# Half of the products of the squares of 16 on GpSimd, one of its folds a step earlier, and the gate's remainders by TensorE and ScalarE

## The chip, the cores and the metric

One core of a Trainium2 chip runs the whole program. The metric is the device time of one execution in microseconds; lower is better. The engines are TensorE (PE in the profile, with its weight loads as PEld), VectorE (DVE), ScalarE (ACT), GpSimd (POOL) and SyncE (SP), whose queue only issues transfers. [...]

## The reference

A block of four layers over x of shape (8, 512, 256) in fp32, each behind a layer norm and added to x:

```
x = x + attn_a(layernorm(x))     # 16 heads of 64; attention inside one token
x = x + ffn(layernorm(x))        # 256 -> 1024 -> 1024 -> 1024 -> 256
x = x + attn_b(layernorm(x))     # 16 heads of 16, causal over the 512 tokens
x = x + ffn(layernorm(x))        # the same weights again
```

Attention A is the unusual part. For every token and head, q, k and v are vectors of 64 numbers, the scores are their outer product, masked causally, and the softmax goes over the 64 channels:

```
scores[q, k] = Q[q] * K[k] / 8,  k <= q        # 64 x 64 for each token and head
attn[q] = sum_k softmax(scores)[q, k] * V[k]
```

No matrix product computes these scores; they are elementwise work. The feed-forward net is `h = silu(x W1) * (x W2)`, two layers with GELU, and W3.

## The kernel before, in words

**Squares.** Tokens lie in the partitions, 128 at a time. The causal triangle of 64 x 64 is cut into squares below the diagonal: one of 32, two of 16, four of 8 and so on, and the diagonal. A *group* is 128 tokens and 4 heads; there are 8 batches x 4 groups of heads x 4 tiles of tokens = 128 groups. A group has four *units*, `u`:

- u=0: the squares of 32 of heads 0 and 1 (tile `w`, three buffers)
- u=1: the squares of 16 of all four heads (tile `w16`, one buffer; the trace names it `w` too)
- u=2: the squares of 32 of heads 2 and 3 (`w`)
- u=3: the squares of 8, 4, 2 and 1 (`ws`, one buffer)

One unit goes through these stages:

- `scores` (L784): the products q*k, 2 x 1024 elements in each partition for u=0, 1, 2. GpSimd makes them for u=0 and 2, VectorE for u=1 and 3.
- `exps` (L798): ScalarE's exponential, one instruction for a unit.
- `weigh` (L808): VectorE multiplies by v into the second half of each part of the tile.
- `halve` (L814): a transfer, issued by GpSimd, adds the second 2048 columns of a tile onto the first 2048 (1024 KB). Not for u=3.
- `fold` (L819): GpSimd adds 1024 columns onto 1024, for u=0 and 2 only.
- `gather` (L845): VectorE's sum over the columns left, into a small tile `red`; for u=1 it reads the 2048 columns themselves.
- `add_rows` (L852): GpSimd adds `red` to the group's accumulator `acc`.

At the end of a group VectorE takes the reciprocal of the denominators (`invert`, L856), GpSimd multiplies (`divide`, L860), and TensorE turns and projects the result.

**Order.** The order on TensorE, VectorE, ScalarE and GpSimd is written out by hand: `AttentionA.step(n)` issues, for step n, the stages of the units n, n-1, n-2 and so on, in three parts with a `yield` after each. So four steps make a group. Counting steps by the unit that begins in them (s0 to s3), `gather` of u=1 stands at the end of part 1 of s1, the `add_rows` for it, `small_squares` and the fold of u=2 follow on GpSimd in part 2 of s1, and `gather` of u=2 stands in part 3 of s2. The fold of u=0 stands in part 2 of the next group's s0, its `gather` in part 3 of s1.

**The other layers.** `after_a` is one long generator with the feed-forward nets and attention B of batch after batch. From step 75 on, when batch 0 has left attention A, some of it is issued after every part of a step. How much is told by the numbers that it yields, against `total` = 309.5 for each batch of 64 steps. So batch b's other layers run beside attention A of batch b+1, and those of batch 7 stand alone at the end. Transfers of the `hidden` and `gate` weights are issued by GpSimd too.

**The gate** of the feed-forward net, for one of eight chunks `m` of 512 tokens: TensorE's products into two PSUM tiles, `silu` on ScalarE (L1028), the product with the second on VectorE (L1031, `times`), then the split into two fp32r halves for the next layer: ScalarE copies the high half (L1035, `high`), GpSimd subtracts for the low one (L1036). `later` puts a function off to the next `flush`. The products of silu have four buffers, taken in turn by `m % 4`.

**The start.** `later_weights` prepares the weights of the later layers in about thirty pieces (`prep`); three of them are issued in every step from n=2. Its last pieces (`bound_scores`) load the Q, K and V weights again and square them on ScalarE (L373, L374). `fit_qkv(1)` to `fit_qkv(3)`, each two products on GpSimd, are issued at the end of steps 0, 1 and 2.

Of the kernel before, what the change touches and what calls it, by code (L numbers as in the profile page):

```python
# [16 lines left out]
P = 128  # L17
# [9 lines left out]
GW = GH * C  # L27
# [257 lines left out]
def fast_path(ctx: ExitStack, tc: tile.TileContext, k, t, flag):  # L285
# [184 lines left out]
    def plus(ps, xi):  # L470

        nc.tensor.matmul(ps, ident, xi, start=False, stop=True)

    rends = const.tile([P, 2, NB], F32, name="rends")
    means = const.tile([P, NB, 2, NT], F32, name="means")

# [127 lines left out]
    class AttentionA:  # L604
# [33 lines left out]
        def step(self, n):  # L638
# [15 lines left out]
                self.x[b] = load_x(b)  # L654
            b, i, g, u = self.at(n + 10)
            if u == 0 and g == 0 and i == 0:
                self.measure(b)
            b, i, g, u = self.at(n + 8)
            if u == 0 and g == 0:
                self.live["xn"] = normed(self.x[b][:, i, :], *self.rn[b, i], "a")  # L660
# [22 lines left out]
            if u == NU - 1:  # L683
                self.small_squares(b, i, g)

            b, i, g, u = self.at(n - 4)
            if u == 0:
                self.fold(b, i, g, u)
            b, i, g, u = self.at(n - 3)
            if u == 2:  # L690
                self.fold(b, i, g, u)
# [14 lines left out]
                self.project(b, i, g)  # L706
            yield
            b, i, g, u = self.at(n - 4)
            if u == 2:
                self.gather(b, i, g, u)  # L710
            b, i, g, u = self.at(n - 5)
            if u == 0:
                self.gather(b, i, g, u)
            b, i, g, u = self.at(n - 3)
            if u == NU - 1:
                self.gather(b, i, g, u)
            b, i, g, u = self.at(n - 7)
            if u == NU - 1:
                nc.scalar.copy(self.live["att"], self.live.pop("pta"))
# [45 lines left out]
        def scores(self, b, i, g, n_u):  # L765

            qv, kt = self.live[b, i, g][:2]
            if n_u == 0:
                acc = ap_.tile([P, 2, GW], F32, tag="acc", name=f"acc_{b}_{i}_{g}", bufs=3)
                self.live[b, i, g].append(acc)  # L770
                nc.vector.tensor_tensor(acc[:, 0, :], qv[:, 0], kt[:, 0], ALU.mult)

            if n_u in (0, 2):
                w = wt.tile([P, 4096], F32, tag="w", name=f"w_{b}_{i}_{g}_{n_u}", bufs=3)
            elif n_u == 1:
                w = wt.tile([P, 4096], F32, tag="w16", name=f"w16_{b}_{i}_{g}")
            else:
                w = wt.tile([P, 2 * SMALL], F32, tag="ws", name=f"ws_{b}_{i}_{g}")
            self.live[b, i, g, n_u] = w
            eng, q = (nc.gpsimd, kt[:, 1]) if n_u in (0, 2) else (nc.vector, qv[:, 0])  # L780
            for n, off, nsq, cols in squares(units[n_u]):
                for e, ev, rows, columns in pieces(w, n, off, nsq, cols):
                    shape = list(e.shape)
                    eng.tensor_tensor(  # L784
                        e, rows(q).to_broadcast(shape), columns(kt[:, 0]).to_broadcast(shape), ALU.mult
                    )
                    yield
# [50 lines left out]
        def gather(self, b, i, g, n_u):  # L838


            w = self.live.pop((b, i, g, n_u))
            for n, off, nsq, cols in squares(units[n_u]):
                if n > 2:
                    red = ap_.tile([P, 2, nsq * n], F32, tag=f"red{nsq * n}", name=f"red_{b}_{i}_{g}_{n_u}_{n}", bufs=2 + (n < 32))
                    nc.vector.tensor_reduce(red, self.columns_of(w, n, off, nsq), AX.X, ALU.add)  # L845
                    self.sums.append((b, i, g, n, cols, red))

        def add_rows(self, b, i, g, n, cols, part):

# [164 lines left out]
    def ffn(u, b, xt, nx, after):  # L1014
# [11 lines left out]
        def gate(m, p1, p2, h):  # L1026
            x = silus[:, m % 4]
            nc.scalar.activation(x, p1, AF.Silu, scale=s_sb[:, 0, m : m + 1])  # L1028

            def times():  # L1030
                nc.vector.scalar_tensor_tensor(x, p2, s_sb[:, 1, m : m + 1], x, ALU.mult, ALU.mult)  # L1031
                later(high)

            def high():
                nc.scalar.copy(h(0, m), x)  # L1035
                later(lambda: nc.gpsimd.tensor_tensor(h(1, m), x, h(0, m), ALU.subtract))  # L1036

            later(times)

        for m0 in range(0, MC, 2):  # L1040
# [30 lines left out]
            for m in (m0, m0 + 1):  # L1071
                p = ps[m - m0] or [ps_f.tile([P, S], F32, tag="pf", name=f"pw{j}_{u}_{m}") for j in range(2)]
                for j in range(2):
                    products(p[j], m, j, last if ps[0] else slice(0, S))
                flush()
                later(lambda m=m, p=p, h=h: gate(m, *p, h))
                yield 0.5 if ps[0] else 1.8
        for _ in range(2):
            flush()
            yield 1  # L1080

# [254 lines left out]


    each = NT * NG * NU
    total = 309.5
    ET = mybir.EngineType  # L1340
    with tc.manual_schedule(engines={ET.PE, ET.DVE, ET.Activation, ET.Pool}):
        a = AttentionA()
        prep = later_weights()
        fit_qkv(0)
        weights = None
        done, spent = after_a(), 0
        for n in range(-10, a.steps):
            for part, _ in enumerate(a.step(n)):
                if n >= 2:
                    next(prep, None)  # L1350
                while 3 * spent * each < total * (3 * (n - each - 11) + part + 1):
                    spent += next(done)
            if 0 <= n < NG - 1:
                fit_qkv(n + 1)
        for _ in done:
            pass
    judge()
# [86 lines left out]
```

## Time and profile before

| | |
|---|---|
| median of 3 runs | 4008.09 us (4007.45 to 4010.71) |
| the profiled execution's own time | 4009.55 us |
| its span | 4007.6 us |
| mean granted TensorE clock | 0.845 |
| busy: DVE, POOL, PE, ACT | 3376.7, 3098.1, 2958.0, 2337.2 us |

The span falls into four stretches. Up to about 150 us the program starts. Up to about 505 us attention A of batch 0 runs alone. Up to about 3690 us attention A of the batches 1 to 7 runs beside the other layers of the batches 0 to 6. The rest is batch 7's other layers. Busy GpSimd time counts its instructions that issue transfers. A row of a timeline is: start, duration, engine, line, operation, tiles, shapes, and in brackets the idle time before it and what ended that.

### The profile page before, as it was taken

To read this page: it belongs to the slowest core of one execution; us is meant where nothing else is said; L and a number is where in the kernel's file an instruction comes from. 1 tells how busy PE (TensorE), PEld (TensorE's weight loads), DVE (VectorE), ACT (ScalarE), POOL (GpSimd) and SP (SyncE) were. 2 spreads that over 40 slices of the span, in tenths; PEclk is the share of its full clock that TensorE was granted. 3 is DMA by queue.
4 is the path that set the end of the run, shared out by engine and by line. 5 is a ranking of instruction groups with operands and counts; after the bars stand their busy time and mean duration, and the time that the engine had idled before them with its cause. 6 is when DMAs were issued, how large, how long until landed. Compare 5 with 4: busy or idle time off the path is not lost.

```text
span 4007.6 us, 37678 instructions
## 1 busy us (share of the span) xinstructions
PE 2958.0 (74%) x12328; PEld 2012.2 (50%) x12328; DVE 3376.7 (84%) x3777; ACT 2337.2 (58%) x3145; POOL 3098.1 (77%) x3051
## 2 busy tenths in 40 slices
PE   1543478777876888768787788768787778768988
PEld 0311145355653656346553566346653556436847
DVE  4899988998889888998989988998889988897115
ACT  2433465666755766666755767567656667555342
POOL 6688888887888887887888888888888878886211
PEclk7555689888987989889897889879898899879999
DMA  8566777668776777668776688668877687767304
GB/s 240 114 141 145 146 182 182 147 161 199 199 162 126 195 188 196 150 147 210 174 192 139 168 198 214 147 131 198 195 181 151 154 199 205 155 133 210 126 29 167
DMA packets 118653, 671.07 MB, mean 167 GB/s; under 512 B 12704, under 2 KB 31915, under 8 KB 43824
## 3 DMA queue, kind: packets, MB, share of 16 engines
q0 software_dynamic: 78336, 570.46, 62.9%
q1 hardware_dynamic: 40112, 98.11, 6.8%
q8 instruction: 100, 1.64, 0.2%
q14 instruction: 105, 0.86, 0.1%
HBM read 255.90 MB, written 9.96 MB: 66 GB/s over the span
## 4 chain that ended last, share of the span: by engine, by line
DVE 38%; PE 16%; POOL 14%; DMA 12%; issue 8%; ACT 8%; POOLq 0%; DVEq 0%; ACTq 0%
DVE red L845 15%; DMA w<-w 12%; DVE w L808 10%; PE ph L1120 5%; ACT w L798 3%; POOL w L819 3%; DVE ws L808 3%; POOL w L784 3%; PE pqkb L1167 3%; DVE ws L784 3%; POOL acc L852 3%; DVE w L784 2%; POOL w L814 2%; DVE acc L856 2%; POOL h L1036 2%
## 5 line engine op out<-in xcount | busy, mean ns | idle before, releaser
L798 ACT ACTIVATE w<-w 128x2048 f32<-128x2048 f32 x384 | 734.2, 1913 | 653.8 <-POOL w L784 440.8
L1120 PE MATMUL ph<-h,hidden 128*128 128x512 f32 x4096 | 1047.9, 412 | 77.4 <-POOL h L1036 45.5
L784 POOL TENSOR_TENSOR w<-k 128x1024 f32<-128x1024 f32 x512 | 1076.2, 2102 | 9.6 <-ACT k L762 9.0
L1120 PEld LDWEIGHTS ph<-h,hidden 128*128 128x128 f32 x4096 | 795.3, 196 | 282.1 <-POOL h L1036 55.9
L808 DVE TENSOR_TENSOR w<-w,qv 128x1024 f32<-128x1024 f32 x768 | 899.8, 1213 | 22.4 <-ACT w L798 22.3
L845 DVE TENSOR_REDUCE red<-w 128x128 f32<-128x1024 f32 (+1 forms) x384 | 601.8, 1567 | 171.6 <-DMA w<-w 94.6
L819 POOL TENSOR_TENSOR w<-w 128x1024 f32<-128x1024 f32 x256 | 643.1, 2512 | 72.5 <-DMA w<-w 71.9
L814 POOL DMA_DIRECT2D w<-w x384 | 337.1, 878 | 339.7 <-issue 134.8
L852 POOL TENSOR_TENSOR acc<-acc,red 128x256 f32<-128x256 f32 (+1 forms) x640 | 471.0, 736 | 152.3 <-DVE red L845 124.5
L845 DVE TENSOR_REDUCE red<-ws 128x256 f32<-128x2048 f32 (+1 forms) x256 | 435.5, 1743 | 0.0
L746 PE MATMUL qv<-wqv,xnta 128*128 128x512 f32 x512 | 299.3, 715 | 89.9 <-DVE ws L808 82.4
L808 DVE TENSOR_TENSOR ws<-ws,qv 128x1024 f32<-128x1024 f32 (+3 forms) x512 | 294.7, 638 | 49.4 <-ACT ws L798 49.4
L1052 PE MATMUL pw<-xnt,gate 128*128 128x512 f32 (+2 forms) x1152 | 298.8, 419 | 24.9 <-ACT silu L1028 18.0
L784 DVE TENSOR_TENSOR w<-qv,k 128x1024 f32<-128x1024 f32 x256 | 301.3, 1219 | 3.6
L784 DVE TENSOR_TENSOR ws<-qv,k 128x1024 f32<-128x1024 f32 (+3 forms) x512 | 299.8, 648 | 0.0
L868 PE MATMUL bank<-ident,acc 128*128 128x128 f32 x256 | 64.3, 341 | 287.5 <-ACT k L761 287.1
L798 ACT ACTIVATE ws<-ws 128x1920 f32<-128x1920 f32 x128 | 231.5, 1809 | 75.3 <-DVE ws L784 74.7
L1052 PEld LDWEIGHTS pw<-xnt,gate 128*128 128x128 f32 x1152 | 227.6, 213 | 82.1 <-ACT silu L1028 22.3
L1229 ACT ACTIVATE eb<-psb 128x256 f32<-128x256 f32 (+3 forms) x512 | 182.2, 443 | 146.6 <-PE psb L1226 146.3
L1146 PE MATMUL pof<-w,h 128*128 128x256 f32 x1024 | 247.9, 396 | 19.4 <-ACT h L1085 19.4
L1085 ACT ACTIVATE h<-ph,s_sb 128x512 fp32r<-128x512 f32 (+1 forms) x256 | 171.1, 688 | 145.9 <-PE ph L1120 144.6
L856 DVE RECIPROCAL acc<-acc 128x256 f32<-128x256 f32 x128 | 223.2, 1744 | 12.3 <-POOL acc L852 12.3
(143 smaller groups left out, 4723.5 us busy)
## 6 DMA issues: line engine op xcount, KB each, us to landing
w<-w POOLq DMA_DIRECT2D x384, 1024.0 KB, 7.7
hidden<-in_h POOLq DMA_DIRECT2D x128, 1024.0 KB, 7.9
gate<-in_w12p POOLq DMA_DIRECT2D x32, 1024.0 KB, 9.0
w<-w_d SPq DMA_DIRECT2D x16, 1024.0 KB, 12.0
wqv<-wqv_d SPq DMA_DIRECT2D x31, 512.0 KB
wo<-in_wo SPq DMA_DIRECT2D x32, 256.0 KB, 7.4
wbqk<-wbqk_d SPq DMA_DIRECT2D x8, 1024.0 KB
w<-in_h SPq DMA_DIRECT2D x8, 1024.0 KB, 7.0
```

The source lines that it names most:

```text
L746: nc.tensor.matmul(qv.rearrange("p j f -> p (j f)"), xnt[:, c, :], wqv[:, c, :], start=(c == 0), stop=(c == DC - 1),)
L784: eng.tensor_tensor(e, rows(q).to_broadcast(shape), columns(kt[:, 0]).to_broadcast(shape), ALU.mult)
L798: nc.scalar.activation(e, e, AF.Exp, scale=C**-0.5)
L808: nc.vector.tensor_tensor(ev, e, columns(qv[:, 1]).to_broadcast(list(e.shape)), ALU.mult)
L814: nc.gpsimd.dma_start(w[:, :2048], w[:, 2048:], accum_op=ALU.add)
L819: nc.gpsimd.tensor_tensor(w[:, :1024], w[:, :1024], w[:, 1024:2048], ALU.add)
L845: nc.vector.tensor_reduce(red, self.columns_of(w, n, off, nsq), AX.X, ALU.add)
L852: nc.gpsimd.tensor_tensor(rows, rows, part.rearrange("p a (x i) -> p a x i", i=n), ALU.add)
L856: nc.vector.reciprocal(acc[:, 0, :], acc[:, 0, :])
L1052: nc.tensor.matmul(pj[:, toks], w[:, m % 4, j, c, :], xs[:, p, c, toks], start=(p == 0 and c == 0), stop=(p == 1 and c == DC - 1),)
L1120: nc.tensor.matmul(pss[j], w[:, j, c, :], h_in(p, c), start=(p == 0 and c == 0), stop=(p == 1 and c == MC - 1),)
L1146: nc.tensor.matmul(po, h(0, c)[:, i * P : (i + 1) * P], w3[:, c, :], start=(c == 0), stop=False)
```

## The change

Five edits.

- **Scores.** Of the two products of the squares of 16, GpSimd makes the first (`p == 0`), VectorE the second. Both still stand in part 2 of s1.
- **Order.** The fold of u=0 moves from part 2 of the next group's s0 to part 3 of s3, its `gather` from part 3 of s1 to part 3 of s0. The sums of u=0 and u=2 share one `red` tile, and one `add_rows` of 256 columns takes the place of two of 128. `red` has one buffer for the squares of 32 (two before) and two for the others together (three before).
- **Gate.** The low half is now made in PSUM: TensorE multiplies x by the identity and the high half by minus the identity into one tile `rest`, and ScalarE copies it out. The gate has one more stage, a flush after each of its two PSUM tiles, and larger yields; `total` becomes 328.9, which is what a batch's yields then add up to.
- **Start.** The moments of batch 0 are measured ahead of the steps. One piece of `prep` is issued in a step, after its third part, from n=3. `fit_qkv(1)` to `(3)` are issued after steps 4, 14 and 24.
- A constant tile `minus`.

```
+    minus = const.tile([P, P], F32R, name="minus")
+    nc.scalar.activation(minus, ident, AF.Copy, scale=-1.0)
...
-            b, i, g, u = self.at(n - 4)
-            if u == 0:
-                self.fold(b, i, g, u)
             b, i, g, u = self.at(n - 3)
             if u == 2:
                 self.fold(b, i, g, u)
...
             b, i, g, u = self.at(n - 4)
-            if u == 2:
-                self.gather(b, i, g, u)
-            b, i, g, u = self.at(n - 5)
-            if u == 0:
+            if u in (0, 2):
                 self.gather(b, i, g, u)
             b, i, g, u = self.at(n - 3)
             if u == NU - 1:
                 self.gather(b, i, g, u)
+            if u == 0:
+                self.fold(b, i, g, u)
...
-            eng, q = (nc.gpsimd, kt[:, 1]) if n_u in (0, 2) else (nc.vector, qv[:, 0])
             for n, off, nsq, cols in squares(units[n_u]):
-                for e, ev, rows, columns in pieces(w, n, off, nsq, cols):
+                for p, (e, ev, rows, columns) in enumerate(pieces(w, n, off, nsq, cols)):
+
+                    on_pool = n == 32 or n == 16 and p == 0
+                    eng, q = (nc.gpsimd, kt[:, 1]) if on_pool else (nc.vector, qv[:, 0])
...
-                    red = ap_.tile([P, 2, nsq * n], F32, tag=f"red{nsq * n}", name=f"red_{b}_{i}_{g}_{n_u}_{n}", bufs=2 + (n < 32))
-                    nc.vector.tensor_reduce(red, self.columns_of(w, n, off, nsq), AX.X, ALU.add)
-                    self.sums.append((b, i, g, n, cols, red))
+                    if n_u != 2:
+                        self.live["red", n] = ap_.tile(
+                            [P, 2, GW // 2], F32, tag=f"red{n // 32}", name=f"red{n}_{b}_{i}_{g}", bufs=1 + (n < 32)
+                        )
+                    red = self.live["red", n]
+                    part = red[:, :, cols.start // 2 : cols.stop // 2]
+                    nc.vector.tensor_reduce(part, self.columns_of(w, n, off, nsq), AX.X, ALU.add)
+                    if n_u != 0:
+                        self.sums.append((b, i, g, n, slice(0, GW), red))
...
             def high():
                 nc.scalar.copy(h(0, m), x)
-                later(lambda: nc.gpsimd.tensor_tensor(h(1, m), x, h(0, m), ALU.subtract))
+                later(low)
+
+            def low():
+                rest = ps_f.tile([P, S], F32, tag="pf", name=f"rest_{u}_{m}")
+                nc.tensor.matmul(rest, ident, x, start=True, stop=False)
+                nc.tensor.matmul(rest, minus, h(0, m), start=False, stop=True)
+                later(lambda: nc.scalar.copy(h(1, m), rest))
...
                 for j in range(2):
                     products(p[j], m, j, last if ps[0] else slice(0, S))
-                flush()
+                    flush()
                 later(lambda m=m, p=p, h=h: gate(m, *p, h))
-                yield 0.5 if ps[0] else 1.8
-        for _ in range(2):
+                yield 1.5 if ps[0] else 2.9
+        for _ in range(3):
             flush()
             yield 1
...
-    total = 309.5
+    total = 328.9
...
+        a.measure(0)
         fit_qkv(0)
...
-                if n >= 2:
+                if n >= 3 and part == 2:
                     next(prep, None)
...
-            if 0 <= n < NG - 1:
-                fit_qkv(n + 1)
+            if n in (4, 14, 24):
+                fit_qkv(n // 10 + 1)
```

More of the change, by code (lines that the diff above doesn't have):

```diff
@@ L656, in step @@
             if u == 0 and g == 0 and i == 0:
-                self.measure(b)
+                if b > 0:
+                    self.measure(b)
             b, i, g, u = self.at(n + 8)
```

## The prediction

> **What bounds the kernel now.** First I read the busy time by stretches (columns: us, then busy us and instructions of PE, PEld, DVE, ACT, POOL, then the granted clock, the DMA share, GB/s).
>
> ```profile
> 150.00:505.00 355.00, 142.24 (x249) 67.26 (x250) 354.38 (x366) 140.00 (x143) 310.05 (x271) 0.56 0.69 142
> 520.00:3690.00 3170.00, 2469.46 (x10498) 1692.99 (x10499) 2845.79 (x3193) 2038.09 (x2731) 2634.06 (x2596) 0.87 0.74 175
> 3690.00:4007.00 317.00, 292.04 (x1416) 217.46 (x1414) 84.08 (x111) 108.74 (x216) 51.68 (x86) 0.98 0.33 112
> ```
>
> While attention A is alone, DVE is busy 354.4 of 355 us and POOL 310. In the long middle DVE is still the fullest (2846 of 3170), with 324 us idle. The tail is PE's. The waits of DVE in the middle stretch say what that idle time is:
>
> ```profile
> DVE red L845 <- DMA w<-w: 87.3, 38, 4.9
> DVE red L845 <- POOL w L819: 76.5, 29, 5.6
> DVE silu L1031 <- ACT silu L1028: 52.4, 24, 5.0
> DVE xnt L983 <- ACT xnt L976: 28.8, 22, 3.4
> ```
>
> Landings of `halve`, folds, and the gate's silu. Last, one group of attention A alone, from the timeline (rows of other engines left out):
>
> ```profile
> 311.24 2.63 POOL L819 TENSOR_TENSOR w<-w 128x1024 f32<-128x1024 f32 x1
> 311.31 2.28 DVE L845 TENSOR_REDUCE red<-w 128x256 f32<-128x2048 f32 x1
> ...
> 313.62 2.36 DVE L784 TENSOR_TENSOR w<-qv,k 128x1024 f32<-128x1024 f32 x2
> 313.73 0.81 POOL L852 TENSOR_TENSOR acc<-acc,red 128x256 f32<-128x256 f32 x1
> 314.42 0.69 POOL L835 TENSOR_TENSOR ws<-ws 128x256 f32<-128x256 f32 x1
> 315.19 1.66 POOL L852 TENSOR_TENSOR acc<-acc,ws 128x256 f32<-128x256 f32 x2
> ...
> 315.90 1.21 DVE L845 TENSOR_REDUCE red<-w 128x128 f32<-128x1024 f32 x1
> ...
> 316.80 2.36 POOL L819 TENSOR_TENSOR w<-w 128x1024 f32<-128x1024 f32 x1
> ...
> 319.61 1.21 DVE L845 TENSOR_REDUCE red<-w 128x128 f32<-128x1024 f32 x1
> ...
> 335.03 2.28 DVE L845 TENSOR_REDUCE red<-w 128x256 f32<-128x2048 f32 x1
> ```
>
> The sum over the squares of 16 (311.31) recurs at 335.03: 23.7 us for a group, DVE without a gap. POOL's fold of u=2 ends at 319.16; DVE sums that tile at 319.61. That handover has 0.45 us to spare, the narrowest place of the loop.
>
> **The skill.** The Trainium skill, "PSUM — Partial Sum Buffer", Engine vs sequencer instructions, says that the queues of ScalarE, VectorE and GpSimd are strict FIFO. The trace agrees: at 313.73 POOL starts on the sum that DVE ended at 313.59, then goes through its part of s1 in written order. "SBUF — State Buffer", Who interferes with whom, says that a DVE instruction with at most one SBUF input does not contend with GpSimd. DVE reads q from PSUM in L784, and its products there average 1.22 us in long stretches with POOL busy all the while; so I charge nothing for the two sharing `w16`.
>
> **The change part by part.**
>
> *1. The product of 16s.* DVE loses 128 x 1.18 = 151 us (301.3 us for 256), 1.13 us start to start in a group. POOL gains 1.9 us (its L784 from start to next start: 319.12 to 321.02). But `w16` has one buffer, and POOL's half is written over columns that DVE's sum of the previous group's 16s reads. So POOL must now wait for that sum, and on POOL's queue behind the product stand the add, `small_squares` and the fold of u=2. The chain from the end of DVE's sum: product 1.9, add 0.7, L835 0.8, two adds 1.6, fold 2.35 = 7.3 us. In that time DVE has its own product 1.2 and the weighing of u=0 2.65 (0.35 + 2.3; the sum of u=0 has moved away) = 3.85 us, then stands before the sum of u=2. New stall: 7.35 - 3.85 = **3.5 us a group** where nothing else fills it. Loop: 7.3 on POOL, then DVE from 319.61 to 337.31 = 17.7, plus the sum of u=0 1.13, plus 0.2 for handovers = 26.4 instead of 23.7, **+2.7 us**.
>
> *2. Fold of u=0 a step earlier, one add for two.* POOL: 0.76 in place of 2 x 0.70, -0.64 a group. The fold leaves the stretch before 311, where POOL afterwards only waits. In s3 it stands three adds behind the transfer of the 16s and some 8 us behind its own transfer; the median landing is 7.7 us. Attention A alone just about covers that. Where `hidden` loads share the queues (landings of 9 to 15 us there), POOL can stand still there and begin the next group's products later. Nothing to +1 us in such groups (about 45 in all). The fewer `red` buffers cost nothing: each is added on POOL before the same DVE sum comes round.
>
> *3. The gate.* POOL loses 179.4 us (L1036), 1.45 for each of 128. With edits 1 and 2 POOL's total stays where it was (+243, -82, -179 = -18 us). PE gains two fp32 records of 512 columns and one fp32r one. In the tail L1167's 512-column records are busy 0.44 us each and L1120's 0.23, so 1.1 us a gate; the tail has 16 gates and PE is full there: **+18 us**. The other 112 are 123 us on a PE that is busy 2469 of 3170, some two groups in each batch at about 96%: between 0 and 123, I take a third, 40. ACT gains 128 copies like L1035 (0.615), 79 us on an engine with over 1100 us free in the middle: nothing, since its queue mostly waits for products. What is won: silu's buffers came free only after POOL's subtraction; the 52 us of silu waits go. The larger yields with the larger `total` only spread the gate (8 x 2.9 of 328.9 over 16 groups is 1.13 groups, where 8 x 1.8 of 309.5 was 0.74), and crowd the rest by 6%. No queue of SP's is passed.
>
> *4. The start.* DVE's longest idle time is there: 24.7 us before a weighing at 112.7, behind ACT's L374, which waits for the `sk` load until 107. With one piece a step, the squaring comes at step 19, a few steps after the load can be issued, and GpSimd's pieces no longer crowd the first group. Between 0 and -45; I take **-28**. The moments of batch 0 (2 us on DVE) are hidden by the load of the weights until 12.9.
>
> *Sum against the profiled execution (4009.55 us; span 4007.6).*
> - Attention A alone: 15 groups x 2.7 = **+40**.
> - Middle, 110 groups of 28.8 us (25.9 busy, 2.9 idle on DVE). Per group: -1.13 of work. The new stall is 3.6 less the DVE work of other layers between the two sums; going through the timeline group by group that is 1.0 on average (0 in six of sixteen groups, up to 2.7 where gates run): +2.6. Not additive with it: the old wait for the fold (76.5/110 = 0.7, the longer of the two counts), silu (0.5 gone), and 0.4 of the waits for landings, since DVE's loop before the sum of 16s grows by the sum of u=0 (1.13 us at about 38 of these waits). Then PE 0.4 and the early fold 0.15. Total +0.42: **+46**.
> - Start -28, tail +18.
>
> Together +76: 4086. That execution is 1.5 above the median of 4008.09, so **4085** as a median. A change under 0.2% (8 us) could not be told from none.
>
> **Rivals.**
> *A, faster (0.21).* In the middle the new stall is hidden in full by the idle time that was there, since a group already waiting for a landing loses nothing by waiting for the fold. For it: groups of about 30 us where DVE works 24 beside `hidden` loads. Against it: about a quarter of the groups run at 23.7 to 26.4 with no idle time to hide it in. If work falls by 1.13 and 0.3 more of idle time goes, the middle gives -1.4 x 110 = -157 at most, and with half of that -78: with +40, -28 and +18 the time is 3880 to 3960, say **3955** as the nearer. It decides from the point where DVE's idle time in a group stays below 3.7 us (2.9 + 1.13 less 30/110); I expect 4.4.
> *B, PE as the bound (0.14).* The added products do not fit beside `hidden`, and all 123 us count, with the folds' waits (+45): 4086 + 83 + 29 = about **4198**. For it: PE at 28 of 29 us in the groups after a gate. Against: 700 us of PE idle in the middle.
> *C, no change (0.06).* Gains in the gate's groups equal the losses elsewhere: 4000 to 4016.
> *D, the edit does not do what it says:* GpSimd gets no lighter, and its load over a group is not evened, because all of it hangs on DVE's sum of 16s. That is part of my main case (0.59), 4030 to 4140.
>
> **How the numbers follow.** Slower holds main case and B: 0.73; same C: 0.06; faster A: 0.21. The range 3955 to 4185 leaves out the lower half of A and the upper part of B, about 2 in 10. Within the main case alone it is 4030 to 4140.
>
> **What would show it.** Right: in attention A alone a group takes about 26.4 us, DVE waits there some 3.5 us before the 128x1024 sum of u=2, released by POOL's fold, and POOL idles ahead of its product of 16s. The waits of DVE list the fold first, with 250 to 400 us; those for silu nearly vanish. The tail is about 18 us longer, the long wait at 112 gone. Wrong: a group alone at 22.6 to 23.7, which would mean that POOL's product does not wait for DVE's sum; or DVE idle under 3.7 us in the middle's groups.

## The result, and the profile after

The changed kernel takes **4255.4 us** (median of 4 runs, 4251.4 to 4258.2), the kernel before 4008.9 beside it: ratio **1.061** (95% interval 1.060 to 1.063), 246 us slower. The prediction was 4085, with a range up to 4185: the sign is right, the size is not.

The same stretches as before, with the tail's moved to where it now lies (columns: us, busy us and instructions of PE, PEld, DVE, ACT, POOL, granted clock, DMA share, GB/s):

```profile
150.00:505.00 355.00, 145.44 (x323) 81.64 (x323) 301.33 (x315) 129.74 (x132) 301.05 (x242) 0.54 0.63 134
520.00:3690.00 3170.00, 2423.05 (x10108) 1635.05 (x10112) 2569.70 (x2904) 2033.29 (x2699) 2530.11 (x2342) 0.89 0.69 165
3940.00:4257.00 317.00, 290.84 (x1362) 208.62 (x1360) 80.94 (x102) 112.95 (x224) 21.96 (x57) 0.97 0.29 99
```

While attention A is alone, VectorE was busy 354 of 355 us and is now busy 301; in the middle its idle time grew from 324 to 600 us. No engine became a bound there: TensorE, ScalarE and GpSimd are each less busy than they were in the same 3170 us.

One group of attention A alone, from the timeline (rows of other engines left out; lines of attention A have moved on, so L845 is now L851, L819 L820, L784 L785):

```profile
311.41 2.29 DVE L851 TENSOR_REDUCE red<-w 128x256 f32<-128x2048 f32 x1
...
313.74 1.22 DVE L785 TENSOR_TENSOR w<-qv,k 128x1024 f32<-128x1024 f32 x1
313.78 1.96 POOL L785 TENSOR_TENSOR w<-k 128x1024 f32<-128x1024 f32 x1 [0.67 <-DVE red L851]
...
315.20 2.35 DVE L809 TENSOR_TENSOR w<-w,qv 128x1024 f32<-128x1024 f32 x2
315.69 0.73 POOL L859 TENSOR_TENSOR acc<-acc,red 128x256 f32<-128x256 f32 x1
316.38 0.62 POOL L836 TENSOR_TENSOR ws<-ws 128x256 f32<-128x256 f32 x1
317.07 1.66 POOL L859 TENSOR_TENSOR acc<-acc,ws 128x256 f32<-128x256 f32 x2
318.69 2.34 POOL L820 TENSOR_TENSOR w<-w 128x1024 f32<-128x1024 f32 x1
...
321.07 1.22 DVE L851 TENSOR_REDUCE red<-w 128x128 f32<-128x1024 f32 x1 [3.52 <-POOL w L820]
...
337.62 2.29 DVE L851 TENSOR_REDUCE red<-w 128x256 f32<-128x2048 f32 x1
```

This is the loop that the prediction drew. GpSimd stands 0.67 us until VectorE's sum of the 16s ends at 313.70, then works through product, add, `small_squares`, two adds and fold; VectorE is done at 317.55 and waits 3.52 us. The sum recurs after 26.2 us, against 23.7.

The waits of VectorE in the middle stretch (a row: who waits <- for whom: us in all, times, the longest; `xnt` is the other layers' normalised x, whose low half VectorE makes behind ScalarE's copy):

```profile
DVE red L851 <- POOL w L820: 248.4, 90, 6.6
DVE silu L1038 <- ACT silu L1035: 92.7, 50, 4.8
DVE xnt L990 <- ACT xnt L983: 79.2, 16, 10.0
DVE w L809 <- ACT w L799: 51.1, 22, 5.1
DVE red L851 <- DMA w<-w: 35.6, 20, 3.1
```

Before, the same rows were 76.5, 52.4, 28.8, 17.2 and 87.3 us. The fold's row was expected. The next three, all waits for ScalarE, were not. In the middle a group now takes 30.69 us, not 28.83.

### The profile page after: what moved, and what is told of

Same layout as the page of the kernel before. It is cut to its first block, busy times and chain, and to the rows that moved or that the text cites. A ratio compares the mean times of both kernels' runs of the same rounds, so it can differ in the third digit from the quotient of the medians.

```text
span 4256.4 us, 38379 instructions
## 1 busy us (share of the span) xinstructions
PE 3090.6 (73%) x12712; PEld 2066.2 (49%) x12712; DVE 3249.4 (76%) x3649; ACT 2465.4 (58%) x3318; POOL 3156.6 (74%) x2923
## 5 line engine op out<-in xcount | busy, mean ns | idle before, releaser
L785 POOL TENSOR_TENSOR w<-k 128x1024 f32<-128x1024 f32 x640 | 1325.3, 2071 | 240.2 <-DVE red L851 221.9
L799 ACT ACTIVATE w<-w 128x2048 f32<-128x2048 f32 x384 | 734.3, 1912 | 812.4 <-POOL w L785 811.5
L1133 PE MATMUL ph<-h,hidden 128*128 128x512 f32 x4096 | 1017.4, 405 | 10.9 <-DMA hidden<-in_h 9.9
L809 DVE TENSOR_TENSOR w<-w,qv 128x1024 f32<-128x1024 f32 x768 | 900.0, 1214 | 56.5 <-ACT w L799 56.5
L851 DVE TENSOR_REDUCE red<-w 128x128 f32<-128x1024 f32 (+1 forms) x384 | 599.7, 1562 | 375.2 <-POOL w L820 336.4
L1133 PEld LDWEIGHTS ph<-h,hidden 128*128 128x128 f32 x4096 | 783.3, 193 | 200.1 <-issue 23.2
L820 POOL TENSOR_TENSOR w<-w 128x1024 f32<-128x1024 f32 x256 | 606.7, 2370 | 50.4 <-DMA w<-w 47.0
L851 DVE TENSOR_REDUCE red<-ws 128x256 f32<-128x2048 f32 (+1 forms) x256 | 435.5, 1743 | 0.0
L859 POOL TENSOR_TENSOR acc<-acc,red 128x256 f32<-128x256 f32 x512 | 408.7, 798 | 27.5 <-DVE red L851 7.6
L1065 PE MATMUL pw<-xnt,gate 128*128 128x512 f32 (+2 forms) x1152 | 305.0, 416 | 26.2 <-DVE xnt L990 13.9
L809 DVE TENSOR_TENSOR ws<-ws,qv 128x1024 f32<-128x1024 f32 (+3 forms) x512 | 299.1, 649 | 10.6 <-ACT ws L799 10.6
L785 DVE TENSOR_TENSOR ws<-qv,k 128x1024 f32<-128x1024 f32 (+3 forms) x512 | 300.0, 650 | 0.0
L745 PEld LDWEIGHTS qv<-wqv,xnta 128*128 128x128 f32 x512 | 107.0, 223 | 308.5 <-issue 228.9
L740 PE MATMUL bank<-wk,xnta 128*128 128x256 f32 x512 | 158.9, 439 | 129.9 <-ACT x L894 108.5
```

Of the source, the lines that this page charges most:

```text
L745: nc.tensor.matmul(qv.rearrange("p j f -> p (j f)"), xnt[:, c, :], wqv[:, c, :], start=(c == 0), stop=(c == DC - 1),)
L785: eng.tensor_tensor(e, rows(q).to_broadcast(shape), columns(kt[:, 0]).to_broadcast(shape), ALU.mult)
L799: nc.scalar.activation(e, e, AF.Exp, scale=C**-0.5)
L809: nc.vector.tensor_tensor(ev, e, columns(qv[:, 1]).to_broadcast(list(e.shape)), ALU.mult)
L820: nc.gpsimd.tensor_tensor(w[:, :1024], w[:, :1024], w[:, 1024:2048], ALU.add)
L851: nc.vector.tensor_reduce(part, self.columns_of(w, n, off, nsq), AX.X, ALU.add)
```

## The experiments

All kernels, each compared with the kernel before on the same chip. *Alone* is the median time of a group while attention A runs alone, *middle* the mean of 96 groups from the 17th on (both from start to start of `invert`), *tail* the time from the last `invert` to the end. The diffs below are cut to the lines that matter, and comments in them are added.

| kernel | median us | ratio (95% interval) | alone | middle | tail |
|---|---|---|---|---|---|
| before | 4009 to 4011 | 1 | 23.72 | 28.83 | 319.2 |
| after | 4255.4 | 1.061 (1.060 to 1.063) | 26.20 | 30.69 | 341.7 |
| noprod | 4131.4 | 1.029 (1.026 to 1.031) | 24.37 | 29.87 | 337.5 |
| oldgate | 4192.9 | 1.045 (1.043 to 1.047) | 26.20 | 30.31 | 320.4 |
| gateonly | 4084.6 | 1.018 (1.016 to 1.021) | 23.72 | 29.30 | 337.8 |
| orderonly | 4056.1 | 1.011 (1.009 to 1.014) | 24.36 | 29.16 | 322.4 |
| startonly | 3996.1 | 0.996 (0.995 to 0.998) | 23.72 | 28.90 | 322.1 |
| second | 4257.3 | 1.060 (1.057 to 1.063) | 26.19 | 30.75 | 341.3 |
| foldfirst | 4357.0 | 1.086 (1.084 to 1.088) | 25.13 | 31.78 | 339.6 |
| prodlate | 4233.2 | 1.055 (1.054 to 1.057) | 24.34 | 30.96 | 320.4 |
| dummy | 4180.4 | 1.042 (1.041 to 1.044) | 24.03 | 30.26 | 319.3 |
| halffold | 4232.6 | 1.055 (1.053 to 1.057) | 26.20 | 30.56 | 337.7 |
| explate | 4307.0 | 1.073 (1.071 to 1.075) | 26.20 | 31.07 | 341.6 |
| paceonly | 4057.3 | 1.011 (1.009 to 1.013) | 23.72 | 29.21 | 324.2 |
| gateoldpace | 4084.4 | 1.019 (1.017 to 1.021) | 23.72 | 29.31 | 339.7 |
| nolow | 3957.7 | 0.987 (0.986 to 0.989) | 23.72 | 28.43 | 319.2 |
| lowpe | 3988.0 | 0.994 (0.993 to 0.996) | 23.72 | 28.58 | 338.8 |
| lowact | 3970.6 | 0.990 (0.988 to 0.992) | 23.72 | 28.50 | 322.2 |
| gatelate | 4107.5 | 1.024 (1.022 to 1.026) | 23.72 | 29.56 | 338.3 |
| lowboth | 4061.8 | 1.013 (1.011 to 1.015) | 23.72 | 29.11 | 340.2 |

### What each edit costs

**noprod**: after, without the moved product.

```diff
-                    on_pool = n == 32 or n == 16 and p == 0
+                    on_pool = n == 32
```

> The changed kernel, but VectorE makes both products of the squares of 16 again. Theory 1 (late products: GpSimd hangs on VectorE's sum of 16s, its products of 32s come late, ScalarE's exponentials wait for them in its queue and silu and the layer norm's copies stand behind them): groups of attention A alone fall back to 23.7 us, waits of VectorE for silu and for xnt fall below 60 us each, time 3960 to 4030. Theory 2 (the rebuilt gate is what costs in the middle stretch): attention A alone at 23.7 too, but the middle stays slow, time 4120 to 4180.

4131.4 us, in the range of the second theory: the product is worth 4255.4 - 4131.4 = 124 us. But a group alone takes 24.37, not the 23.7 that both had:

```profile
304.44 1.22 DVE L851 TENSOR_REDUCE red<-w 128x128 f32<-128x1024 f32 x1 [0.54 <-POOL w L820]
```

The order edit took the sum of u=0 (1.13 us) out of the stretch that covered GpSimd's fold. The 0.45 us to spare became 0.54 us of waiting.

**oldgate**: after, with the gate of before (the diff's gate edit undone, with its flush, yields and `total`). **gateonly**: before, with that edit alone.

> The changed kernel with the gate of before: GpSimd subtracts for the low half, one flush for a chunk, the old yields and total = 309.5. Theory 1: the waits for silu stay at 100 us or more and attention A alone at 26.2 us a group; time 4200 to 4290, the tail some 18 us shorter. Theory 2: the excess of the middle goes, time 4060 to 4110.

> The kernel before with nothing but the new gate (TensorE and ScalarE make the low half, a flush after each PSUM tile, the larger yields, total = 328.9). Theory 1: the tail is about 18 us longer, the middle a little shorter or the same since silu's buffers come free earlier: 3970 to 4040. Theory 2: the middle is slower by some 100 to 160 us: 4120 to 4190.

The gate is worth 62 us taken back and 74 put in, which lies between the two expectations of gateonly; 19 to 21 of them are the tail (341.7 against 320.4; 337.8 against 319.2). In gateonly VectorE's wait for silu over the whole run rises from 55 to 112 us, that for `xnt` from 48 to 80; without the new gate silu still takes 108. So both the gate and the rest of the change make silu late, each by itself.

**orderonly** and **startonly**: before, with one of these edits of the diff.

> Before, with the order edit alone (fold of u=0 a step earlier, its sum moved, one add for two). Theory (it takes a sum of 1.13 us out of the cover of the fold of u=2, and in the middle that is as dear as a load): 24.3 us a group alone, 0.5 to 0.7 us more a group in the middle, 4070 to 4090 us. Rival (it costs only together with the moved product): middle within 0.2 us, 4015 to 4040 us.

> Before, with the start edit alone (moments of batch 0 ahead of the steps, one piece of the weights' preparation a step, the three fits after steps 4, 14 and 24). Theory: the gain of the start seen in every kernel that has the edit (first reciprocals 12 and 39 us earlier) stays, and nothing else moves: 3975 to 3992 us, ratio 0.992 to 0.996. Rival (the preparation's later pieces run into the middle and give it back): 4000 to 4015 us.

Order: about +45 us, between the two expectations (0.64 us a group alone as the theory had it, 0.33 in the middle where it had 0.5 or more). In the middle stretch the wait for folds rises from 76.5 to 135.4 us and that for landings falls from 87.3 to 30.8, about the same sum. The price lies in ScalarE's rows again, which were 52.4, 28.8 and 13.2:

```profile
DVE red L848 <- POOL w L817: 135.4, 83, 7.3
DVE silu L1035 <- ACT silu L1032: 64.4, 34, 5.0
DVE xnt L987 <- ACT xnt L980: 38.8, 21, 3.5
DVE red L848 <- DMA w<-w: 30.8, 18, 2.8
DVE h L1095 <- ACT ph L1091: 25.2, 28, 2.4
```

Start: 0.4% faster, about 15 us, a little less than the theory had. Group 17 begins 20 us earlier, and some of that is given back. This is the only edit of the five that pays; alone it makes the best full version here. The four pieces nearly add up: 124 + 74 + 45 - 15 = 228 of 246 us.

### The loop of the squares of 16

**second**: GpSimd takes the second product in place of the first, so that VectorE's product, not GpSimd's, lies first in the tile.

```diff
-                    on_pool = n == 32 or n == 16 and p == 0
+                    on_pool = n == 32 or n == 16 and p == 1
```

> The changed kernel with one character changed: GpSimd makes the second product of the squares of 16 (columns 2048 to 3072 of w16), which VectorE's sum does not read, so GpSimd has to wait for the landing of halve alone. Theory 1: the product is out of the way before the sum ends, the chain after the sum is 5.4 us against 3.85 of VectorE's own, so the stall before the sum of u=2 is about 1.6 instead of 3.5 us and a group of attention A alone takes 24.2 to 24.6 us; products come earlier, the waits for silu shrink by half or more; time 4000 to 4070. Theory 2: the stall shrinks in the same way but the middle keeps its other waits: 4130 to 4200.

Nothing changed (26.19 alone), against both theories. GpSimd waits as before:

```profile
313.63 1.95 POOL L785 TENSOR_TENSOR w<-k 128x1024 f32<-128x1024 f32 x1 [0.66 <-DVE red L851]
```

By the layout in `pieces`, the sum reads the columns 0 to 2047 of the tile, and this product goes to 2048 to 3071. So GpSimd waits for the sum although none of the columns that it writes is read there. This suggests that the wait is for the one buffer of `w16` as a whole, not for columns; a second buffer was not tried.

**foldfirst**: as second, with GpSimd's product issued behind the fold of u=2 (in part 2 of s1).

```diff
             if u == 2:
                 self.fold(b, i, g, u)
+            for _ in rest:      # the product p == 1 of the 16s
+                pass
```

> The changed kernel with GpSimd's product of 16s (the second of the two, as in the run before) put behind the fold of u=2 in its queue; same work everywhere. If the place of the product in GpSimd's chain is what its part costs: the chain from VectorE's sum of 16s to the end of the fold falls from 7.3 to 5.4 us against 3.85 us of VectorE's own, so the stall is 1.5 to 2 us, a group of attention A alone 24.2 to 24.8 us, and the time 4080 to 4140, about that without the moved product. If it is GpSimd's added load, wherever it stands: a group alone stays at 25.5 to 26.2 us and the time is 4200 to 4260.

The chain to the fold gets shorter, as meant: alone 25.13 us, and a wait of 1.66 (with one row of ScalarE).

```profile
332.58 2.28 DVE L856 TENSOR_REDUCE red<-w 128x256 f32<-128x2048 f32 x1
...
340.30 3.86 POOL L790 TENSOR_TENSOR w<-k 128x1024 f32<-128x1024 f32 x2
340.37 1.22 DVE L856 TENSOR_REDUCE red<-w 128x128 f32<-128x1024 f32 x1 [1.66 <-POOL w L825]
...
342.28 1.91 ACT L804 ACTIVATE w<-w 128x2048 f32<-128x2048 f32 x1 [6.50 <-POOL w L790]
```

And the time is 102 us worse than after, outside both expectations. The late product makes its own exponential late: the one of the 16s starts at 342.28, 9.7 us after the start of VectorE's sum of the group before. In after this was 4.4 us (311.41 to 315.77):

```profile
315.77 1.91 ACT L799 ACTIVATE w<-w 128x2048 f32<-128x2048 f32 x1 [1.40 <-POOL w L785]
```

Also, two products now follow each other behind the fold, so the transfer after them is issued 3.8 us after the fold's end, where second has 1.9. VectorE's wait for silu over the whole run goes to 165 us, that before the weighing of `w` to 123 (129 and 57 in after). Shortening the loop that is seen alone does not help the middle.

**prodlate**: before with the start edit and that late product; old order and old gate.

> The kernel before with the change's start, and with the second product of 16s on GpSimd behind the fold of u=2; old order of the folds and old gate. If the place in the chain is what counts: VectorE loses 1.13 us of work a group and gains no stall, a group of attention A alone takes 22.6 to 23.3 us, the time is 3920 to 3980, of which some 35 us come from the start. If GpSimd's load counts: a group alone at 24 us or more, time 3990 to 4050.

4233 us, 237 more than startonly and outside both expectations. Alone a group takes 24.34 us, more than startonly's 23.72, though VectorE has 1.1 us less to do. So taking the product out of the fold's way does not make it cheap. But load and place are not told apart here: as in foldfirst the exponential of the 16s comes late, 9.7 us after the sum's start alone (4.75 in startonly) and 11.3 in the middle (6.4). VectorE's waits over the whole run spread over ScalarE's work (in this order 86, 39, 22, 56 and 27 us in startonly):

```profile
DVE red L852 <- POOL w L826: 150.1, 84, 6.1
DVE h L1098 <- ACT ph L1094: 115.6, 47, 8.6
DVE w L815 <- ACT w L805: 101.9, 53, 5.6
DVE silu L1038 <- ACT silu L1035: 98.7, 38, 5.2
DVE ws L815 <- ACT ws L805: 82.9, 43, 5.0
```

### Is it GpSimd's load as such?

**dummy**: before, with work on GpSimd behind the fold of u=2 that nobody reads.

```diff
+            if unit[3] == 1:
+                self.spare(*unit)
...
+            for x in (0, 4):     # two products of 512 into a spare tile
+                nc.gpsimd.tensor_tensor(e, a.to_broadcast(shape), c.to_broadcast(shape), ALU.mult)
```

> Before, with two products of 512 elements added on GpSimd behind the fold of u=2 in part 2 of s1, about 2.2 us a group; their result is read by nobody, and nothing else is changed. Theory (GpSimd is nearly full beside the other layers, and any work added to it makes its products of 32s late, then ScalarE's exponentials, then what is queued behind them): most of what the product cost behind the fold (+2.1 us a group in the middle) comes back, 1.2 to 2.2 us a group there, 4140 to 4250 us, with VectorE's waits for folds, silu and ScalarE's copies up. Rival (the load alone is harmless, only what waits for the moved product counts): within 0.4 us a group, 4010 to 4055 us. Alone: GpSimd has 20.7 of 23.7 us a group busy, so up to 0.6 us there under both.

The page's group of these products (busy us, mean ns, idle us before them):

```profile
L831 POOL TENSOR_TENSOR spare<-k 128x512 bf16<-128x512 f32 x256 | 274.1, 1071 | 10.0
```

274 us of work without a reader, 2.14 in a group, cost **169 us**: 0.31 a group alone, 1.43 in the middle, as the theory had it. VectorE's waits in the middle stretch (87.3, 52.4, 76.5 and 28.8 before):

```profile
DVE red L857 <- DMA w<-w: 157.6, 58, 7.1
DVE silu L1043 <- ACT silu L1040: 75.4, 35, 5.0
DVE red L857 <- POOL w L821: 67.6, 36, 5.5
...
DVE xnt L995 <- ACT xnt L988: 42.6, 20, 3.4
```

The wait for folds fell, against the theory, and the one wait for GpSimd that grew is small (the layer norm's moments, 1.9 to 14.2 us). What grew are the landings and ScalarE's silu, copies and exponentials (those of `ws` from 24.4 to 48.2). Over the whole run ScalarE waits 579 us for GpSimd's products, 441 before. All of VectorE's waits for landings stand before the sum of the 16s. Counted from the trace over the middle's 96 groups, GpSimd issues the `halve` of u=0 4.3 us after its last weighing (2.2 before). The `halve` of u=1, issued almost as promptly as before (0.8 us, 0.6 before), then follows it after 5.5 us in place of 7.1 and takes 10.0 us to land in place of 8.7. So the load is dear even where nobody waits for its result.

**halffold**: after, with the fold of u=0 cut to half its columns.

```diff
+            k = 512 if n_u == 0 else 1024
-            nc.gpsimd.tensor_tensor(w[:, :1024], w[:, :1024], w[:, 1024:2048], ALU.add)
+            nc.gpsimd.tensor_tensor(w[:, :k], w[:, :k], w[:, 1024 : 1024 + k], ALU.add)
```

> After, with the fold of u=0 cut to 512 columns onto 512 (half of that addition is left out): about 1.2 us a group less on GpSimd at a place that has time to spare before its sum, nothing else changed. Theory (GpSimd's load as such counts): alone 26.2 us a group as in after, in the middle 0.5 to 1.0 us a group less, 4145 to 4200 us. Rival (only the chain from the sum of the 16s through GpSimd's product to the fold of u=2 counts): within 0.2 us a group, 4235 to 4260 us.

23 us less, and 0.13 a group in the middle, for 140 us less on GpSimd (folds 606.7 to 466.4). The theory's 0.5 a group is out; the rival's group time came, with a total 2 us below its range. GpSimd's products in after, then in halffold:

```profile
L785 POOL TENSOR_TENSOR w<-k 128x1024 f32<-128x1024 f32 x640 | 1325.3, 2071 | 240.2 <-DVE red L851 221.9 <-ACT k L761 17.6
```

```profile
L785 POOL TENSOR_TENSOR w<-k 128x1024 f32<-128x1024 f32 x640 | 1324.9, 2070 | 356.4 <-DVE red L852 338.7 <-ACT k L761 17.0
```

Of 140 us saved, 117 come back as more waiting for VectorE's sum. In after, a load ahead of the waiting product is nearly free: what is saved there goes into the wait. GpSimd's load has no single price.

### Is it the order in ScalarE's queue?

**explate**: after, with the exponentials issued in part 2 of a step, so that the other layers' work goes ahead of them.

```diff
-            if self.at(n - 1)[0] is not None:
-                self.exps(*self.at(n - 1))
             yield
...
+            if self.at(n - 1)[0] is not None:     # behind the folds of part 2
+                self.exps(*self.at(n - 1))
```

> After, with the exponential of the unit n-1 issued in part 2 of a step and no longer at the end of part 1, so that ScalarE's pieces of the other layers issued after part 1 go ahead of it. Theory (silu and the copies are late because they stand behind an exponential that waits for GpSimd's product): ScalarE's wait for the products falls from 811 us to under 600, VectorE's waits for silu and xnt (234 us together) to under 150, and the time to 4150 to 4220 us. Rival (nothing is won at ScalarE's head, the exponential itself only comes later): VectorE's wait for the exponential before the weighing (57 us) grows over 150, 4255 us or more.

52 us slower than after. The first half of the theory came: ScalarE's wait for products falls from 811.5 to 648. The second did not (whole run):

```profile
DVE red L851 <- POOL w L820: 337.3, 109, 8.1
DVE silu L1038 <- ACT silu L1035: 133.4, 77, 4.1
DVE xnt L990 <- ACT xnt L983: 117.0, 31, 15.1
```

silu and `xnt` wait 250 us, not under 150 (234 in after). VectorE's waits before the weighing of `w` and `ws`, for the later exponentials, rise from 56.5 + 10.6 to 69.3 + 45.5 us: 48 us, the largest change, the rival's way, though no single row reached its 150. So that an exponential waiting at ScalarE's head holds up silu behind it is not the mechanism, or not one that this reordering can free.

### Why is the gate edit dear?

**paceonly**: before, with the larger yields and the third flush of the edit, and nothing of its work. **gateoldpace**: the edit with the small yields of before.

```diff
-                yield 0.5 if ps[0] else 1.8
-        for _ in range(2):
+                yield 1.5 if ps[0] else 2.9
+        for _ in range(3):
...
-    total = 309.5
+    total = 328.9
```

> The kernel before with the larger yields of the gate, a third flush at its end and total = 328.9; GpSimd still subtracts, no added work. If the gate's part of the loss (74 us) is a matter of pace (other layers are issued 6% denser, so the layer norm's chains and their waits fall on other places of a step): 4060 to 4090, with longer waits of VectorE for xnt. If it is the new stages on TensorE and ScalarE: 3995 to 4015.

> The kernel before with the new gate on TensorE and ScalarE and its flushes, but the old yields (total 311.5, for the one added flush). If pace is the cause: 4015 to 4035, of which 18 us are the tail's. If the stages on TensorE and ScalarE are: 4060 to 4100.

The pace alone costs 47 us, the work at the old pace 74, both together (gateonly) 74. The larger yields bring longer waits for `xnt` and before the weighing of `w`: over the whole run 79.4 and 45.0 us in paceonly, 47.6 and 22.3 before, 44.5 and 24.8 in gateoldpace. Beside the new work the pace costs nothing more, since silu then waits less (112.3 us in gateonly, 146.1 in gateoldpace). So it is the work that was taken apart. In **nolow** the low half is left out, so that only GpSimd's relief is left; **lowpe** adds TensorE's two products to that, **lowact** ScalarE's copy.

```diff
-                later(lambda: nc.gpsimd.tensor_tensor(h(1, m), x, h(0, m), ALU.subtract))
+                later(low)             # lowpe: the two products into rest, not copied
+                later(lambda: later(lambda: nc.scalar.copy(h(1, m), x)))     # lowact
...
+                h_in = lambda p, m, h=h: h(0, m)      # all three
```

> Before, with the gate's low half left out: GpSimd's subtraction (1.45 us for each of 128 gates) is not done, and the next layer's products read the high half twice, so TensorE's work is as before. It is the gate edit's relief for GpSimd alone, without what TensorE and ScalarE get in exchange. Theory (GpSimd's load counts at the rate that the products read by nobody showed, about 0.65 us of time for 1 us of work, in both directions): 0.6 to 1.1 us a group less in the middle, 3890 to 3950 us; the gate edit then cost some 150 us on TensorE and ScalarE. Rival (the relief is worth nothing, since these subtractions lie where GpSimd waits anyway): 3990 to 4020 us, and the gate edit cost 74 in all.

> As the last one, with the gate edit's two products into PSUM for the low half added on TensorE in their stage, not copied out and read by nobody. Its difference to the last one is TensorE's share of the gate edit: 141 us of instructions, 18 of them in the tail. Theory (TensorE is the dear part, its gates' stretches being full): 60 to 110 us above the last one. Rival (TensorE's 700 idle us in the middle hide it outside the tail): 15 to 40 us above.

> As the one without the low half, with one more copy of the product on ScalarE (from SBUF, 128 of 0.6 us) in the stage where the gate edit has its copy out of PSUM, read by nobody. Its difference to that one is ScalarE's share. Theory (a copy more in ScalarE's queue makes the next silu and the layer norms' copies late): 40 to 90 us above it. Rival (ScalarE has over 1100 us free in the middle): within 15 us.

GpSimd's relief: -52 us for 179 us less work, between the two expectations. (ScalarE's and TensorE's waits for that subtraction, 43.0 and 45.5 us before, go with it.) TensorE: +30, of which 338.8 - 319.2 = 20 are the tail, so 10 in the middle (the rival). ScalarE: +13 (the rival). These give 4001; the edit is at 4084. So 83 us belong to neither part alone. Two runs, both changes to gateoldpace, looked for them: **gatelate** puts the copy off by a flush, **lowboth** makes it from the product in SBUF.

```diff
-                later(lambda: nc.scalar.copy(h(1, m), rest))
+                later(lambda: later(lambda: nc.scalar.copy(h(1, m), rest)))     # gatelate
+                later(lambda: nc.scalar.copy(h(1, m), x))                       # lowboth
```

> Before, with the gate edit at the old pace, and the copy of the low half out of PSUM issued one flush later than in the edit, so that other work of ScalarE's stands between TensorE's two products and the copy that waits for them (one flush more at the end of a gate loop, its yield in the total). Theory (the gate edit is dear because ScalarE stands at the head of its queue before that copy until TensorE is done, 3 to 4 us in two groups of a batch, with the next silu behind it): VectorE's wait for silu falls from 146 us to 50 to 80, the time from 4084 to 4005 to 4040 us, near the sum of the two parts taken alone (52 saved, 30 and 13 paid). Rival (the two parts simply add up to more than each alone, or the PSUM tile of the low half is held longer and TensorE lacks a bank for the next products): 4075 us or more.

> Before, with the gate edit at the old pace, and its last copy made from the product in SBUF in place of the PSUM tile (the low half is then not the remainder). TensorE's products, ScalarE's copy, the stages and the flushes all stay as in the gate edit; what goes is that ScalarE waits for TensorE's low half and that a PSUM tile, one of five, is held until that copy. Theory (the link is what is dear: a PSUM tile more for each gate, held through a wait): 3990 to 4030 us, near 3958 with 30 and 13 added. Rival (the work of both at once, or the flush after each PSUM tile, is dear in itself): 4060 us or more.

gatelate: ScalarE's wait for TensorE falls from 71.6 to 31.6 us, and the time rises by 23. TensorE now waits before the low half, rows that were under 18 us each:

```profile
PE rest L1042 <- ACT silu L1030: 58.6, 28, 3.9
...
PE rest L1042 <- DVE silu L1033: 39.5, 15, 3.2
```

lowboth: 22 us less than gateoldpace, as its rival had it, VectorE's wait for silu 107.6 in place of 146.1. Holding the PSUM tile longer costs 23, not holding it for ScalarE saves 22, so the link is worth that much; that TensorE's wait is one for a free PSUM tile is argued, not shown. The other 61 us stay with the work of both engines together, and with the flush after each PSUM tile, which nolow, lowpe and lowact do not have. No run separates the two, but the code and the traces show what that flush does. Before, a chunk's `yield` stands between the silu and VectorE's product of it, so work of attention A can be issued between them; with the flush none can. Between the start of the silu and that product VectorE starts 1.5 other instructions in the mean before, and 0.4 in gateoldpace and lowboth. Without the flush VectorE waits 26 to 56 us for silu (before, nolow, lowpe, lowact, paceonly), with it 108 to 146 (gateonly, gateoldpace, gatelate, lowboth). That the next layer's products wait for a later low half is not seen: TensorE has no such wait in gateoldpace.

## Why the prediction was wrong, step by step

| step | predicted us | measured us |
|---|---|---|
| attention A alone, 15 groups | +40 | 15 x 2.48 = +37 |
| start | -28 | about -20 at group 17, -15 in all |
| tail | +18 | 341.7 - 319.2 = +22.5 |
| middle, 110 groups | 0.42 x 110 = +46 | 1.86 x 110 = +205 |

**Right.** The loop through GpSimd: 26.4 us expected, 26.2 measured, a stall of 3.5 against 3.52, with the releaser named. (The reason given, columns that the sum reads, cannot be the whole of it: second writes none of them and waits alike.) The Trainium skill's strict FIFO ("PSUM — Partial Sum Buffer", Engine vs sequencer instructions) carries that reading, and this trace agrees at 313.78. The tail, too: lowpe shows TensorE's products at 20 us there. Rival A, that the middle hides the stall, is out. Rival B gave 4198, nearer to the result, by a mechanism that the runs refute: TensorE's share of the middle is about 10 us, not 123 (nor the 40 that the sum took). The 40 rested on "some two groups in each batch at about 96%"; counted from `invert` to `invert`, only five groups of the middle are above 95%. B's sum does not close either: with all 123 and the 45 for the folds it comes to 4208.

**Wrong: the middle term.** For a group of VectorE, busy and idle time in the middle stretch (3170 us are 110.0 groups before and 103.3 after):

| us a group | before | after | measured | predicted |
|---|---|---|---|---|
| work | 25.88 | 24.88 | -1.00 | -1.13 |
| wait for folds | 0.70 | 2.40 | +1.71 | +2.6 - 0.7 = +1.9 |
| wait for landings | 0.79 | 0.34 | -0.45 | -0.4 |
| wait for silu | 0.48 | 0.90 | +0.42 | -0.5 |
| wait for `xnt` | 0.26 | 0.77 | +0.50 | none |
| wait before the weighing of `w` | 0.16 | 0.49 | +0.34 | none |
| other, and PE 0.4 and early fold 0.15 | 0.56 | 0.91 | +0.34 | +0.55 |

The stall in the middle, the step that looked the least certain, came within 0.2. Two steps failed.

*"The 52 us of silu waits go"*: they grew, 0.92 us a group from what was said, some 100 us. The wait that this was read from did go. Before, ScalarE stood ahead of silu for GpSimd's subtraction; no kernel with the new gate has such a row:

```profile
ACT silu L1028 <- POOL h L1036: 43.0, 30, 3.5
```

And with the subtraction alone left out (nolow), VectorE's wait for silu falls to half of its 55.0 us:

```profile
DVE silu L1031 <- ACT silu L1028: 26.1, 17, 2.3
```

But the new gate issues VectorE's product right behind the silu, and the wait comes back larger (112 us in gateonly, 146 in gateoldpace). Taking GpSimd off saves 52 us in all (nolow); the stages and the flush put in its place cost 126.

*"The larger yields with the larger `total` only spread the gate"*: they were priced at nothing. The waits for `xnt` and before the weighing of `w` (0.84 a group, 92 us) were not in the sum at all, and they come with these yields: paceonly, which changes nothing else but a flush at the gate's end, has them at 79.4 and 45.0 us over the whole run, after at 105.1 and 56.5, and oldgate, which is after with the old gate and its yields, at 60.1 and 24.1. The two steps together are more than the 159 us by which the middle was missed. That ScalarE's added copies cost *"nothing"* was nearly right (lowact: 13 us).

Beside both stands *"with edits 1 and 2 POOL's total stays where it was"*. Totals do not cancel. Work of 2.1 us a group behind the fold costs 169 us with no reader (dummy); 1.4 us a group taken from the gate gives 52 (nolow); 1.1 us taken ahead of the new wait gives 23 (halffold). By edit, the sum had about 81 us for the product (40 alone; 1.13, 2.6, 0.7 and 0.4 in the middle), 7 for the gate (18 + 44 - 55) and 17 for the order; the runs have 124, 74 and 45.

**Open.** How GpSimd's lateness reaches VectorE. That load alone does it is shown (dummy), and so is the first step, ScalarE's wait for GpSimd's products (441 us before, 579 in dummy, 811 in after). How it goes on from ScalarE to silu and `xnt` is not: reordering the exponentials did not free them (explate). That `halve`, issued late, makes the next transfer's landing later fits the issue times in dummy; it was not tried apart. Nor was the gate's flush without its work, which leaves the 61 us undivided.

## What to carry to other kernels

Cost a moved instruction in two parts: the loop that it closes, which a stretch where the stage runs alone shows to a tenth of a us, and the delay that it brings to everything behind it on its new engine, products and transfers alike, which here cost up to 0.6 us for each us of work that nobody waited for. Relief somewhere else on the same engine does not pay for it: look where the load stands relative to a wait. And a wait that "goes" because its releaser is lighter stays away only if the new order still leaves work between the two instructions, so count what stands between them. A change of pace moves waits too, even where it adds no work.

## What was not expected of the hardware

GpSimd's time has no fixed price on the path: 274 us more cost 169 (0.62 for one), 179 us less gave 52 (0.29), 140 us less gave 23 (0.16). A fold of 1024 columns took 2.36 us, one of 512 columns 1.28 (halffold), so half the size took a little more than half the time. VectorE's product of the squares of 16 kept its 1.22 us (1219 ns in the mean before, 1223 after) while GpSimd wrote the other half of the same tile, as the prediction had assumed.
